# Issuing the value rows' product before the bias rows' product, so that another engine empties the PSUM buffer that q's product takes

## The chip, the cores and the metric

One core of one Trainium2 chip runs the whole kernel. The metric is the device time of one execution in microseconds. The kernel before has a median of 4380.1 us over 3 runs (4376.23 to 4390.58).

## The reference: what is computed

The input `x` has shape (2, 128, 256, 256). One layer does two things to it.

```python
x = x + conv_ref(ln_over_channels(x), W_qkv, W_out, rel_height, rel_width)
t = to_tokens(x)
t = t + ffn_ref(ln_over_channels(t), router_w, router_b, expert_w, expert_b)
x = from_tokens(t)
```

`conv_ref` is windowed attention with 4 heads of 32 channels. q, k and v are 1x1 projections. Each window of 8x8 queries sees 12x12 keys around it. A fixed mask of minus infinity keeps only the pairs whose offset is even in both directions, so the image falls apart into four planes (even and odd rows, even and odd columns) that never mix. The scores get a relative position bias made of q times two small tables. After the softmax the result goes through `W_out`. `ffn_ref` is a mixture of 8 linear experts: a softmax router picks the best two for each token, and the token's output is their weighted sum.

## The kernel before, in words

**Tiling.** A strip is 8 image rows, and there are 64 strips in the two images. A strip has 4 planes of 512 queries, so a main loop of 256 planes (`for n in range(n_planes + 7)`) does nearly all the work. In step `n` the loop scores, attends and projects plane `n`, prepares plane `n + 1` (function `project`, called `ahead` in the loop), and runs the expert layer and the norms for image rows of neighbouring strips. The order of the work on all engines is written out by hand under `tc.manual_schedule`; each engine takes its instructions in that order.

**The TensorE order of one step**, with the lines of the profile: bias scores and q-k scores of plane n (L474, L491); then for plane n + 1 the bias rows `pu` (L408), the value rows `pv` (L350), the key rows `pk` (L423) and q `pq` (L445); four expert products (L714); softmax sums and attention (L512, L522); norm statistics `plt` (L580); three expert products; the output projection `po` (L550); one more expert product; then padding NOPs (L823) that fill the instruction stream to a multiple of 256, and the next step.

**PSUM buffers.** `pu`, `pv`, `pk`, `pq`, `plt`, `plg` and `po` all come from `mm_tile`, a pool of 3 buffers that are handed out in turn. In nearly all steps there are seven of them, so each takes the buffer of the third before it and must wait until that one has been read. In the first strip of each image the value and key rows come in two parts each, which makes nine.

| tile | read by | who next takes its buffer, before |
|---|---|---|
| `pu` | VectorE transpose to `uT`, L413 | `pq` |
| `pv` | ScalarE copy to `vr`, L358 | `plt` |
| `pk` | ScalarE copies to `kcol`, L434 and L441 | `plg` (written by VectorE, L589) |
| `pq` | ScalarE copy to `qs`, L447 | `po` |
| `plt` | VectorE transpose to `plg`, L589 | the next `pu` |
| `plg` | VectorE, last in L621 | the next `pv` |
| `po` | VectorE add, L555 | the next `pk` |

**The VectorE order of one step**, from `uT`: `uT` (L413), two shifted copies and a transpose (L392, L397), `xs` (L699), six expert multiplications (L705), the sum of the finished experts (L720, reads `acc`), softmax sums `sT` (L532, waits for L522), reciprocal, `rT`, `o` (L542), `plg` (L589), the norm chain (L232 to L235, a round trip through ScalarE, L238, L239), the residual add (L555), the router (L613 to L645), and the gate transpose `gT` (L651), which stands just ahead of the next `uT`.

**GpSimd** does, once in a step, a copy that ties it to VectorE's work (L709), an expert multiplication (L705), the norm of one row pair (L276, needs `rb` from a DMA), in every fourth step the halo copy (L250), and a second expert multiplication (L705).

**ScalarE and SyncE, around the change.** ScalarE's order is the router's exponential (L618), a one-element copy into `gb` for expert 5 (L686), the softmax exponential (L499), `vr` (L358), a one-element copy into `gb` for expert 7 (L686), `kcol` (L434, L441), `qs` (L447), and squares (L574). The one-element copies in L686 pace the DMA queue: the DMA that fills `gb` (L689) cannot be issued before its copy is done. SyncE issues nearly all DMAs, in order: `gb` of experts 5 and 7 (L689), `gd` from `gT` (L659), `vrows` from `vr` (L369), `rb` (L665, reads what `gd` wrote), `sb` (L694), `vwin` (L381), and further `gb` loads.

Of the kernel before, what the change touches and what calls it, by code (L numbers as in the profile page):

```python
# [51 lines left out]
def kernel(  # L52
# [39 lines left out]
    def mm_tile(name):  # L92
        return ps_mm.tile([P, 512], F32, tag="mm", name=name)
# [148 lines left out]
    def ln_rows(i):  # L242

        s = strips[i][1]
        return range(1 if s == 0 else 2, KR - 1 if s == NS - 1 else KR)
# [13 lines left out]
    def runs(i, rows):  # L259

        out = []
        for k in rows:
            if out and place(i, k) == out[-1][1] + out[-1][2]:
                out[-1][2] += 1
            else:
                out.append([k, place(i, k), 1])
        return out
# [71 lines left out]
    def value_rows(n):  # L339

        i, pl = divmod(n, 4)
        xp = xn[i % 2][:, pl // 2, pl % 2]
        rows, sent = list(ln_rows(i)), []
        for part in (rows[-4:], rows[:-4]):
            if not part:
                continue
            pv = mm_tile(f"pv{n}_{part[0]}")
            m = len(part)
            for j, k in enumerate(part):
                nc.tensor.matmul(  # L350
                    pv[:, j * P : (j + 1) * P],
                    lhsT=xp[:, k, 1 : PC + 1],
                    rhs=wv,
                    start=True,
                    stop=True,
                )
            vr = work.tile([P, 4, P], F32, tag="vr", name=f"vr{n}_{part[0]}")
            nc.scalar.copy(  # L358
                vr[:, 0:m].rearrange("p r c -> p (r c)"), pv[:, : m * P]
            )  # L360
            sent.append((part, vr))
        return sent
# [23 lines left out]
    def shift(uT, n, state):  # L386

        for j in range(2):
            shifted = uT[:, :, :, NU * j + 3 : NU * j + 9]
            dims = [list(d) for d in shifted.ap]  # L390
            dims[1 + j][0] -= 1
            nc.vector.tensor_copy(  # L392
                auT[n % 2][:, :, :, 6 * j : 6 * j + 6],
                bass.AP(shifted.tensor, shifted.offset, dims),
            )
        au = work.tile([P, 2 * NP, PR, 4], F32, tag="au", name=f"au{n}")
        nc.vector.transpose(au.rearrange("p m a s -> p a s m"), auT[n % 2])  # L397
        state["au"] = au

    def project(n, state):  # L400

        i, pl = divmod(n, 4)
        xp = xn[i % 2][:, pl // 2, pl % 2]
        inner = xp[:, 1 : 1 + PR, 1 : PC + 1]
        kk = kcol[pl]

        pu = mm_tile(f"pu{n}")
        nc.tensor.matmul(pu, lhsT=wrel, rhs=inner, start=True, stop=True)  # L408
        state["sent"] = value_rows(n)
        yield  # L410

        uT = work.tile([P, PR, 4, 32], F32, tag="uT", name=f"uT{n}", bufs=1)
        nc.vector.transpose(uT, pu.rearrange("p (a m s) -> p a s m", a=PR, s=4))  # L413
        state["shift"] = lambda: shift(uT, n, state)
        yield

        rows = list(ln_rows(i))
        for part in (rows[-4:], rows[:-4]):
            if not part:
                continue  # L420
            pk = mm_tile(f"pk{n}_{part[0]}")
            m = len(part)
            nc.tensor.matmul(  # L423
                pk[:, : m * PC],
                lhsT=wk,
                rhs=xp[:, part[0] : part[0] + m, 1 : PC + 1],
                start=True,
                stop=True,
            )
            pk3 = pk[:, : m * PC].rearrange("p (r c) -> p r c", r=m)  # L430
            for k, at, m in runs(i, part):
                new = pk3[:, k - part[0] : k - part[0] + m]
                places = kk[:, :, 0:NK].rearrange("p t (c r) -> p t r c", r=KR)[:, :, at : at + m]
                nc.scalar.copy(places[:, 1 : NP - 1], windows(new[:, :, KC - 3 :], 0, NP - 2))  # L434

                ends = [places[:, 0, :, 1:], new[:, :, 0 : KC - 1]]
                for j, step in enumerate(((NP - 1) * SLOT - KR, PC - KC + 1)):
                    dims = [list(d) for d in ends[j].unsqueeze(1).ap]
                    dims[1] = [step, 2]
                    ends[j] = bass.AP(ends[j].tensor, ends[j].offset, dims)  # L440
                nc.scalar.copy(*ends)  # L441
        yield

        pq = mm_tile(f"pq{n}")
        nc.tensor.matmul(pq, lhsT=wq, rhs=inner, start=True, stop=True)  # L445
        qs = work.tile([P, 2 * NP, PR, 4], F32, tag="qs", name=f"qs{n}")
        nc.scalar.copy(  # L447
            qs.rearrange("p m a s -> p a m s"), pq.rearrange("p (a m s) -> p a m s", a=PR, s=4)
        )
        yield  # L450

        state.update(qs=qs, kk=kk, vv=vwin[n % 2])
        yield

    def windows(rows, n0, count):

        first = rows[:, :, 8 * n0 : 8 * n0 + KC].unsqueeze(1)
        dims = [list(d) for d in first.ap]
        dims[1] = [8, count]
        return bass.AP(first.tensor, first.offset, dims)  # L460
# [317 lines left out]
    for _ in project(0, states[0]):  # L778
        pass
# [28 lines left out]
    with tc.manual_schedule(engines={ET.PE, ET.DVE, ET.Activation, ET.Pool, ET.SP}):  # L808
        for n in range(n_planes + 7):
# [6 lines left out]
            if n + 1 < n_planes:  # L816
                states[n + 1] = {}
                ahead = project(n + 1, states[n + 1])
# [143 lines left out]
```

## Time and profile before

| | |
|---|---|
| median of 3 runs | 4380.1 us |
| the profiled execution, device time | 4380.58 us |
| its span, first to last instruction | 4378.8 us |
| granted TensorE clock, mean | 0.993 |
| TensorE matmul busy, share of the span | 97% |
| TensorE weight loads busy | 56% |
| VectorE busy | 88% |
| ScalarE busy | 33% |
| GpSimd busy | 25% |
| DMA queue q1, share of 16 engines' span | 74.8% |

The durations in this document are from that one profiled execution, which is within 0.5 us of the median. Busy shares are means over the span. The end of a matmul in a profile is modelled, and matmuls overlap, so a busy TensorE row can hide idle time. A wait in the view of waits is a stretch in which an engine stood idle, with the instruction that let it go on.

### The profile page before, as it was taken

The numbers are of one execution on the slowest core, as the hardware profiler recorded it, in microseconds if no ns is written. First come the engines' busy times: TensorE is split into PE (matmuls) and PEld (weight loads), VectorE is DVE, ScalarE is ACT, GpSimd is POOL, SyncE is SP. The second block draws the span as 40 slices with busy tenths as digits, with TensorE's granted clock in tenths as the row PEclk, the third lists the DMA queues.
The fourth block names the chain that finished last, engine by engine and source line by source line (L and its number), as shares of the span: only waits on it lengthen the run. The fifth ranks groups of instructions, "written<-read, shape, count | busy, mean of one in ns | idle before, by whom it ended". The sixth has DMA issues, their size and how long they took to land. (4 is left out here: it accounts for less than half of the span.)

```text
span 4378.8 us, 224652 instructions
## 1 busy us (share of the span) xinstructions
PE 4248.2 (97%) x94273; PEld 2454.2 (56%) x94273; DVE 3853.9 (88%) x11850; ACT 1456.6 (33%) x3774; POOL 1091.6 (25%) x1126
## 2 busy tenths in 40 slices
PE   7899999999999999999999999999999999999987
PEld 5455555555555555555555555555555555555553
DVE  5899889899888989989888889988998888999987
ACT  3333333333333333333333333333333333333321
POOL 1222222222222222222222222222222222222211
PEclk9999999999999999999999999999999999999999
DMA  4677778777777787777777787777777777777766
GB/s 114 210 240 240 244 235 243 241 237 244 233 244 240 244 244 233 243 232 244 238 241 234 240 244 236 243 236 243 238 240 243 236 242 232 244 238 239 243 191 191
DMA packets 824580, 1022.19 MB, mean 233 GB/s; under 512 B 137634, under 2 KB 409634, under 8 KB 823594
## 3 DMA queue, kind: packets, MB, share of 16 engines
q1 hardware_dynamic: 822864, 1007.52, 74.8%
q8 instruction: 769, 12.60, 1.2%
q14 instruction: 217, 1.78, 0.1%
q10 hardware_dynamic: 730, 0.29, 0.0%
HBM read 863.78 MB, written 143.75 MB: 230 GB/s over the span
## 5 line engine op out<-in xcount | busy, mean ns | idle before, releaser
L714 PE MATMUL acc<-xe,ew 128*128 128x512 f32 x4096 | 1916.8, 600 | 21.4 <-DVE gb L688 17.5
L714 PEld LDWEIGHTS acc<-xe,ew 128*128 128x128 f32 x4096 | 757.9, 190 | 941.4 <-issue 872.1
L705 DVE TENSOR_TENSOR xe<-xs,gb 128x512 f32<-128x512 f32 x1536 | 950.5, 686 | 11.8 <-DMA gb<-gd 1.4
L709 POOL COPY last<-xe 128x1 f32<-128x1 f32 x256 | 47.0, 184 | 3088.0 <-DVE gb L688 3081.0
L705 POOL TENSOR_TENSOR xe<-xs,gb 128x512 f32<-128x512 f32 x512 | 650.7, 1272 | 0.7 <-issue 0.5
L276 POOL TENSOR_TENSOR xn<-xt,rb 128x512 f32<-128x512 f32 x249 | 373.7, 1501 | 170.4 <-DMA rb<-gd 164.1
L491 PE MATMUL att<-qs,kcol 32*64 32x32 f32 x32768 | 398.2, 227 | 5.1 <-issue 5.1
L491 PEld LDWEIGHTS att<-qs,kcol 32*64 32x64 f32 x32768 | 395.9, 131 | 6.6 <-issue 6.2
L522 PEld LDWEIGHTS att<-pT,vwin 64*32 64x32 f32 x32768 | 350.2, 105 | 50.4 <-issue 11.8
L522 PE MATMUL att<-pT,vwin 64*32 64x32 f32 x32768 | 350.6, 200 | 8.0 <-issue 6.3
L350 PEld LDWEIGHTS pv<-wt,xn 128*128 128x128 f32 x2048 | 270.1, 192 | 126.5 <-issue 78.7
L434 ACT COPY kcol<-pk 128x560 f32<-128x560 f32 (+2 forms) x344 | 319.0, 927 | 52.8 <-PE pk L423 49.4
L499 ACT ACTIVATE pT<-att 128x1024 f32<-128x1024 f32 x256 | 261.8, 1023 | 208.0 <-PE att L491 207.2
L445 PE MATMUL pq<-xn,wt 128*128 128x512 f32 x512 | 274.7, 617 | 30.0 <-DVE uT L413 26.0
L574 ACT ACTIVATE sq<-xt 128x512 f32<-128x512 f32 x505 | 291.9, 629 | 0.0
L408 PE MATMUL pu<-xn,wrel 128*128 128x512 f32 x512 | 291.7, 651 | 0.0
L397 DVE STREAM_TRANSPOSE au<-auT 128x512 f32<-128x512 f32 x256 | 272.3, 1064 | 9.0
L550 PE MATMUL po<-o,wt 128*128 128x512 f32 x512 | 264.4, 598 | 8.4 <-DVE o L542 5.8
L350 PE MATMUL pv<-wt,xn 128*128 128x128 f32 x2048 | 271.2, 275 | 0.8 <-issue 0.8
L532 DVE STREAM_TRANSPOSE sT<-att 128x512 f32<-128x512 f32 x256 | 183.5, 717 | 98.7 <-PE att L522 84.7
L423 PE MATMUL pk<-xn,wt 128*128 128x512 f32 (+2 forms) x528 | 262.9, 582 | 1.3 <-DVE uT L413 1.3
L474 PEld LDWEIGHTS att<-au,keys 32*64 32x64 f32 x8192 | 117.9, 133 | 227.8 <-PE po L550 183.5
(2696 smaller groups left out, 4895.9 us busy)
## 6 DMA issues: line engine op xcount, KB each, us to landing
gb<-gd SPq DMA_DIRECT2D x2048, 256.0 KB, 5.8
vwin<-vrows SPq DMA_DIRECT2D x512, 240.0 KB, 5.4
xt<-in_x_dram SPq DMA_DIRECT2D x256, 256.0 KB, 6.6
sb<-gd SPq DMA_DIRECT2D x256, 256.0 KB, 4.1
out_dram<-xt SPq DMA_DIRECT2D x256, 256.0 KB, 6.2
rb<-gd SPq DMA_DIRECT2D x249, 256.0 KB, 3.4
vrows<-vr SPq DMA_DIRECT2D x168, 256.0 KB, 3.9
vrows<-vr SPq DMA_DIRECT2D x160, 128.0 KB, 3.5
```

The source lines that it names most:

```text
L276: eng.tensor_tensor(xn[i % 2][:, :, :, k, 1 : PC + 1], ln1_src(i, k).rearrange("p (y j x) -> p y x j", y=2, x=2), rb.rearrange("p (y j x) ...
L350: nc.tensor.matmul(pv[:, j * P : (j + 1) * P], lhsT=xp[:, k, 1 : PC + 1], rhs=wv, start=True, stop=True,)
L397: nc.vector.transpose(au.rearrange("p m a s -> p a s m"), auT[n % 2])
L408: nc.tensor.matmul(pu, lhsT=wrel, rhs=inner, start=True, stop=True)
L434: nc.scalar.copy(places[:, 1 : NP - 1], windows(new[:, :, KC - 3 :], 0, NP - 2))
L445: nc.tensor.matmul(pq, lhsT=wq, rhs=inner, start=True, stop=True)
L491: nc.tensor.matmul(sc[rows, h, 32 * t : 32 * t + 32], lhsT=kk[hp, half * HP + t, :], rhs=qs[hp, m0 : m0 + 2].rearrange("p m a s -> p (m a ...
L522: nc.tensor.matmul(av[hp, half, 32 * t : 32 * t + 32], lhsT=vv[rows, t, hp], rhs=pT[rows, h, 32 * t : 32 * t + 32], start=True, stop=True,)
L550: nc.tensor.matmul(po, lhsT=wo, rhs=state["o"].rearrange("p f z -> p (f z)"), start=True, stop=True)
L574: nc.scalar.activation(sq, src, AF.Square)
L705: eng.tensor_tensor(self.xe[e], self.xs, self.gb.pop(e), ALU.mult)
L714: nc.tensor.matmul(self.acc, lhsT=ew[:, e, :], rhs=self.xe.pop(e), start=(e == 0), stop=not self.xe)
```

## The change

`project` issues the four value-row products, and the ScalarE copy of them that `value_rows` issues, ahead of the bias rows' product. Nothing else is changed: every instruction is still there, with the same operands, and all other instructions keep their order on their engines.

```diff
@@ project
+        state["sent"] = value_rows(n)
         pu = mm_tile(f"pu{n}")
         nc.tensor.matmul(pu, lhsT=wrel, rhs=inner, start=True, stop=True)
-        state["sent"] = value_rows(n)
         yield
```

The turn of the buffers moves with the order of the tiles. Now `pv` takes the buffer of the previous step's `plt`, `pu` that of `plg`, `pk` that of `po` as before, `pq` that of `pv`, and `plt` that of `pu`. In the first strip of an image, with nine tiles, `pq` still takes the buffer of `pu`.

## The prediction

> **What bounds the kernel now.** I read the shares first. The page's first part names two candidates:
>
> ```profile
> PE 4248.2 (97%) x94273; PEld 2454.2 (56%) x94273; DVE 3853.9 (88%) x11850; ACT 1456.6 (33%) x3774; POOL 1091.6 (25%) x1126
> ```
>
> PE looks full, but the view of waits shows both engines waiting for each other (columns: total us, times, longest):
>
> ```profile
> PEld pq L445 <- DVE uT L413: 176.7, 235, 2.0
> DVE sT L532 <- PE att L522: 84.7, 150, 3.7
> POOL xn L276 <- DMA rb<-gd: 164.1, 116, 30.5
> ```
>
> Neither bounds alone. q's product waits for VectorE's `uT`, and later in the step `sT` waits for TensorE's attention. I then took the starts of the rows of 240 middle planes; from `uT` to `uT` they need 16.65 us on average.
>
> TensorE waiting for nothing: q to L512 4.38, to L522 0.455, to its end 1.34, to `po` 3.62, to L474 1.81, scores 2.015, bias and value rows 1.855 (less 0.07 overlap), keys 0.86: **16.27**. Small holes that are no wait for another engine (ahead of L512 7.9 us, in L522 15.7, in L491 8.5, over 240 planes) make it **16.40**.
>
> VectorE waiting for nothing: `uT` to the end of L720 7.02, to `sT` 0.12, `sT` to the next `uT` 8.97: **16.11**. But that last stretch is 0.32 longer on average (call it e). Nearly all of e is in L235, which takes 0.16 us alone and up to 1.25. Its row shows why; here is one plane, by time (start us, us, engine, line):
>
> ```profile
> 728.33 0.58 ACT L358 COPY vr<-pv 128x512 f32<-128x512 f32 x1 [0.92 <-PE pv L350]
> 728.48 0.67 DVE L413 STREAM_TRANSPOSE uT<-pu 128x512 f32<-128x512 f32 x1
> 728.81 0.19 ACT L686 COPY gb<-onesm 128x1 f32<-128x1 f32 x1
> ...
> 729.45 1.21 SPq L659 DMA_DIRECT2D gd<-gT  x2
> ...
> 733.11 0.33 SPq L665 DMA_DIRECT2D rb<-gd  x1
> ...
> 736.71 1.51 POOL L276 TENSOR_TENSOR xn<-xt,rb 128x512 f32<-128x512 f32 x1 [0.29 <-DMA rb<-gd]
> ...
> 738.17 1.27 POOL L705 TENSOR_TENSOR xe<-xs,gb 128x512 f32<-128x512 f32 x1
> ...
> 738.99 0.47 DVE L235 SCALAR_TENSOR_TENSOR u__42_13603<-u__42_13603,epsc 128x8 f32<-128x8 f32 x1
> ```
>
> L235 ends with POOL's L705 (739.46 and 739.44): POOL is late, because `rb` was late, because `gd` was issued at 729.45 although `gT` was done at 728.55. SP takes its DMAs in order, and ahead of `gd` stands the `gb` of expert 7, which waits for ScalarE's copy behind `vr`. SP's own waits say the same for the whole span:
>
> ```profile
> SPq L689 <- ACT gb L686: 852.2, 525, 16.0
> SPq L659 <- DVE gT L651: 39.6, 11, 11.5
> ```
>
> `gd` hardly ever waits for `gT`. So `vr`, and thus `pv`, sets when `rb` comes.
>
> **What the Trainium skill says.** *Perfetto Trace Analysis*, Identifying the Most-Contended Engine: matmul busy time is no measure of TensorE's headroom, weight loads are better. The trace agrees: 97% against 56%, and the PE row hides most of q's wait. *SBUF — State Buffer*, Who interferes with whom: a VectorE instruction with two SBUF inputs and a GpSimd one that reads SBUF exclude each other for the whole instruction. L235 agrees (0.16 to 1.25 us, ending with POOL). *Perfetto Trace Analysis*, Identifying Dependency Chains: an instruction that waits for several engines may get an event-semaphore instruction ahead of it. `po` has that (255 of 51 ns).
>
> **The loop as it stands, checked.** If TensorE leads the pace, attention ends, `sT` follows after 0.14, and `uT` 8.97 + e later; from the scores' end s this is s + 1.67 + e. q starts 0.73 after `uT` began and, started cold, needs 13.73 to the next s. So the next s is s + 16.13 + e, against 16.27 by TensorE alone: VectorE delays TensorE when e passes 0.14. The mean of what passes is 0.24, and 16.40 + 0.24 = **16.64**; measured 16.65. The account closes.
>
> **The change, part by part.**
>
> *q no longer waits for `uT`.* q then waits for `vr`. That copy can start when the softmax exponential ends, s + 1.2, and ends near s + 1.8; q's turn is at s + 2.65. No wait, with 0.8 to spare. The stall itself, q's start less its turn, was 43.7 us over 240 planes, and the cold start 0.11 in half of them: 12.3. That is 0.23 per plane or 60 us at most. The cold weight load now falls on `pv`, where `pu` paid it before: nothing.
>
> *`pu` moves behind `pv`.* Eight products of 0.11 put it 0.89 later: it starts at s + 0.82, ends near s + 1.95, and `uT` starts not before s + 2.0. Before, 58% of the planes had `uT` under 0.93 after `pu`, so here is the price: a new wait at L413. What is queued behind it is VectorE's whole chain to `sT`. Taken alone it is 0.16 per plane on average. It does not add where TensorE leads, since `sT` waits less by as much.
>
> *The new loop.* VectorE from `uT` s + 2.0 reaches `o`'s end 9.62 later. NOPs follow `o`: first at 0.16, 31 of them in 2.26, then 0.07 to the scores and 2.015 to their end, so s is not before `uT` + 14.13. With `uT` = s + 1.84 + e in a late plane, the next s is s + 15.97 + e. VectorE now delays TensorE only when e passes **0.30** instead of 0.14.
>
> *`vr` comes 0.9 earlier*, and with it, on ScalarE and SP, the copy for expert 7, its `gb`, and `gd`. `gd` was issued on average 1.08 after `uT`'s start; now `gT` holds it, about 0.3. The same trace shows what that is worth: in the 47 planes where `gd` went out within 0.79 of `uT`'s start, POOL waited 0.08 for `rb`, in the others 0.47. The `vrows` DMA stands behind `gd` and moves with it; `rb`, `sb`, `vwin` follow, none later than before.
>
> *e afterwards.* `sT` is hardly late any more, so e has to be taken from the earliest `sT`. For those 47 planes it is then 0.10 without the halo copy and 0.64 with it (every fourth plane), and what passes 0.30 is 0.03 and 0.34. Mean 0.75 x 0.03 + 0.25 x 0.34 = 0.11.
>
> *Edits at no cost.* `plt` now waits for `uT` as well as for ScalarE's squares, so I expect an event semaphore there; at 51 ns it is between nothing and 13 us over 256 planes. I take nothing, since TensorE's sequencer runs ahead there, and one padding NOP less (71 ns) returns it. `pu` waits for L621, which ends 2.6 before `uT`, as `pv` did. `pv` waits for L589, over 4 us earlier, as `pu` did. The 8 planes with nine tiles keep q's wait. The holes in TensorE wait for nothing that the trace shows, so I can't say that they stay; 32 us in all, they may grow or shrink by a sixth: plus or minus 5 us.
>
> *Sum.* 16.40 + 0.11 = 16.51 against 16.65: 0.14 x 256 = 36 us. From the profiled execution's 4380.6 (0.5 from the median): **4345 us**.
>
> **The rivals.**
>
> - *TensorE sets the pace alone.* Halo planes are absorbed too: 16.40, 0.24 x 256 = 62, so 4318. For: all of q's stall goes. Against: 0.64 passes 0.30. Chance 0.2.
> - *No change.* `gd` is earlier, but `rb` only partly, since the DMA engines are 75% full. If half of the planes behave like the early ones and half like the late ones (0.37 passes 0.30 there, from the earliest `sT`), it is 0.5 x 0.11 + 0.5 x 0.37 = 0.24, the loss of before: 4380. Chance 0.13.
> - *Slower, by GpSimd's end.* `rb` does not come earlier at all. With `sT` no longer late, L235 reaches POOL sooner and waits longer, and the wait for `pu` comes on top. What passes 0.30, over all 236 planes with POOL rows, would be 0.31 in place of 0.24: 0.055 x 256 = 14, so 4394. It decides from the point where over half of the planes have `rb` as late as now. For: `rb` follows `gd`'s issue by 2.7 us with a wide spread. Against: the 47 planes. Chance 0.17.
> - *It doesn't do what it says* is only true of the 8 planes with nine tiles.
>
> My forecast has 0.5. **Range**: 4318 to 4394 reaches to the cases at both ends and takes in the event semaphores and the holes; beyond it lie about half of each end case, some 2 in 10. A difference of 0.3% (13 us) is about what this measurement tells from none. Faster 0.5 + 0.2 = 0.7, same 0.13, slower 0.17.
>
> **What would show it.** Right: q's waits for `uT` nearly gone (under 20 us); `sT` <- L522 under 30; a new `uT` <- `pu` of 20 to 60 beside the 35 at the start; SP's wait for ScalarE's `gb` down by over 100 and its wait for `gT` up; POOL's `rb` wait under 90; L235 long only in every fourth plane; 255 or so event semaphores at L580. Wrong: POOL's wait for `rb` as before, or q waiting for `vr`, or larger holes ahead of L512.

## The result: 56 us less, and the profile after

The kernel after takes 4323.6 us (median of 4 runs, 4316.7 to 4327.1) against 4379.5 us of the kernel before, run on the same chip (4 runs). The ratio is 0.9866, with a 95% interval of 0.9844 to 0.9888. The profiled execution took 4321.7 us (span 4319.9) at a granted clock of 0.992.

The direction came as forecast, and so did what frees q and what makes `gd` early. The size did not: the gain was 56 us, where the forecast had 36 and the rival "TensorE sets the pace alone" 62.

The page's first part, after:

```profile
PE 4217.3 (98%) x94273; PEld 2466.8 (57%) x94273; DVE 3852.5 (89%) x11850; ACT 1452.8 (34%) x3774; POOL 1086.0 (25%) x1126
```

The instructions are the same in number. VectorE's busy time differs by 1.4 us and ScalarE's by 3.8. TensorE's matmul row is 30.9 us shorter with as many products, which fits a row that had hidden a part of q's wait. So the gain lies in waits. The view of waits, after (total us, times, longest):

```profile
PEld pq L445 <- issue: 115.4, 480, 0.3
POOL xn L276 <- DMA rb<-gd: 74.6, 15, 29.7
DVE uT L413 <- PE pu L409: 63.6, 39, 13.9
...
DVE sT L532 <- PE att L522: 16.3, 19, 2.3
...
ACT vr L358 <- PE pv L350: 9.7, 8, 4.4
```

- q's weight load no longer waits for `uT` (176.7 us before). What is left has no releaser: 480 gaps of about a quarter of a microsecond, nearly two in each step.
- `sT` waits 19 times for the attention, where it waited 150 times.
- GpSimd's waits for `rb` fell from 116 to 15.
- The forecast price is there too: `uT` now waits 63.6 us for `pu`, 28 more than before.
- `vr` no longer waits for `pv` (241.0 us before, in 254 planes). It starts when ScalarE is free.

The lines of before for the last two points:

```profile
ACT vr L358 <- PE pv L350: 241.0, 254, 5.2
...
DVE uT L413 <- PE pu L408: 35.3, 13, 12.3
```

SyncE's waits, after:

```profile
SPq L689 <- ACT gb L686: 784.2, 675, 14.5
...
SPq L659 <- DVE gT L651: 54.1, 59, 9.7
```

`gd` (L659) is held by `gT` in 59 steps, where it was held in 11. The step that the prediction showed, by time (start us, us, engine, line):

```profile
725.35 1.02 PE L409 MATMUL pu<-xn,wrel 128*128 128x512 f32 x2
...
725.55 0.58 ACT L358 COPY vr<-pv 128x512 f32<-128x512 f32 x1
...
726.03 0.19 ACT L686 COPY gb<-onesm 128x1 f32<-128x1 f32 x1
...
726.28 0.24 DVE L651 STREAM_TRANSPOSE gT<-g 128x64 f32<-128x64 f32 x1
...
726.66 1.43 SPq L659 DMA_DIRECT2D gd<-gT  x2
...
734.37 1.50 POOL L276 TENSOR_TENSOR xn<-xt,rb 128x512 f32<-128x512 f32 x1
...
735.84 1.26 POOL L705 TENSOR_TENSOR xe<-xs,gb 128x512 f32<-128x512 f32 x1
...
736.75 0.38 DVE L235 SCALAR_TENSOR_TENSOR u__42_13603<-u__42_13603,epsc 128x8 f32<-128x8 f32 x1
```

`vr` is copied while `pu` is computed. So ScalarE's copy for expert 7 is done at 726.22, before `gT` (726.52), and `gd` goes out 0.14 after `gT`, where it was 0.90. GpSimd's L276 then shows no wait for `rb`, and L235 takes 0.38 in place of 0.47, although it still ends with GpSimd's L705 (737.13 and 737.10).

From the row starts of 236 middle planes, as means: `gd` goes out 0.18 after `uT`'s start (1.13 before), GpSimd waits 0.04 for `rb` (0.38), and a plane takes 16.386 us (16.65). That is 0.264 x 236 = 62 us; the span is 59 us shorter, so the planes at the two ends gained nothing.

### The profile page after: what moved, and what is told of

It is laid out like the page before. It is cut to its first block, busy times and chain, and to the rows that moved or that the text cites. A ratio compares the mean times of both kernels' runs of the same rounds, so it can differ in the third digit from the quotient of the medians.

```text
span 4319.9 us, 224653 instructions
## 1 busy us (share of the span) xinstructions
PE 4217.3 (98%) x94273; PEld 2466.8 (57%) x94273; DVE 3852.5 (89%) x11850; ACT 1452.8 (34%) x3774; POOL 1086.0 (25%) x1126
## 5 line engine op out<-in xcount | busy, mean ns | idle before, releaser
L714 PE MATMUL acc<-xe,ew 128*128 128x512 f32 x4096 | 1915.4, 600 | 18.6 <-DVE gb L688 16.5
L705 DVE TENSOR_TENSOR xe<-xs,gb 128x512 f32<-128x512 f32 x1536 | 950.6, 686 | 11.1 <-DMA gb<-gd 1.1
L705 POOL TENSOR_TENSOR xe<-xs,gb 128x512 f32<-128x512 f32 x512 | 650.6, 1272 | 1.5 <-PE att L522 0.7
L491 PE MATMUL att<-qs,kcol 32*64 32x32 f32 x32768 | 400.6, 226 | 11.1 <-issue 10.8
L491 PEld LDWEIGHTS att<-qs,kcol 32*64 32x64 f32 x32768 | 396.7, 131 | 13.9 <-issue 13.6
L276 POOL TENSOR_TENSOR xn<-xt,rb 128x512 f32<-128x512 f32 x249 | 373.7, 1501 | 91.1 <-DMA rb<-gd 74.6
L522 PEld LDWEIGHTS att<-pT,vwin 64*32 64x32 f32 x32768 | 348.6, 105 | 40.8 <-issue 3.2
L522 PE MATMUL att<-pT,vwin 64*32 64x32 f32 x32768 | 345.1, 200 | 2.4 <-issue 2.2
L350 PE MATMUL pv<-wt,xn 128*128 128x128 f32 x2048 | 301.1, 291 | 0.9 <-issue 0.9
L409 PE MATMUL pu<-xn,wrel 128*128 128x512 f32 x512 | 266.2, 602 | 1.2 <-issue 1.2
L445 PE MATMUL pq<-xn,wt 128*128 128x512 f32 x512 | 261.9, 592 | 0.9 <-issue 0.8
L350 PEld LDWEIGHTS pv<-wt,xn 128*128 128x128 f32 x2048 | 251.7, 193 | 11.8 <-issue 1.3
L474 PEld LDWEIGHTS att<-au,keys 32*64 32x64 f32 x8192 | 118.9, 132 | 234.0 <-PE po L550 181.1
L413 DVE STREAM_TRANSPOSE uT<-pu 128x512 f32<-128x512 f32 x256 | 177.1, 692 | 65.5 <-PE pu L409 63.6
```

The lines of the kernel that those rows point to most:

```text
L276: eng.tensor_tensor(xn[i % 2][:, :, :, k, 1 : PC + 1], ln1_src(i, k).rearrange("p (y j x) -> p y x j", y=2, x=2), rb.rearrange("p (y j x) ...
L350: nc.tensor.matmul(pv[:, j * P : (j + 1) * P], lhsT=xp[:, k, 1 : PC + 1], rhs=wv, start=True, stop=True,)
L491: nc.tensor.matmul(sc[rows, h, 32 * t : 32 * t + 32], lhsT=kk[hp, half * HP + t, :], rhs=qs[hp, m0 : m0 + 2].rearrange("p m a s -> p (m a ...
L522: nc.tensor.matmul(av[hp, half, 32 * t : 32 * t + 32], lhsT=vv[rows, t, hp], rhs=pT[rows, h, 32 * t : 32 * t + 32], start=True, stop=True,)
L705: eng.tensor_tensor(self.xe[e], self.xs, self.gb.pop(e), ALU.mult)
L714: nc.tensor.matmul(self.acc, lhsT=ew[:, e, :], rhs=self.xe.pop(e), start=(e == 0), stop=not self.xe)
```

## The experiments

The theory to test was that the gain needs **both** things that the new order brings, q's product free of `uT`, and `vr`, thus `gd` and `rb`, early. The two rivals were that one of them alone is enough. A further question was what sets the pace now. All ratios are to the kernel before on the same chip (medians there 4377.2 to 4379.5).

The readings, as means or sums over 236 middle planes. The last two columns are the gaps in TensorE ahead of two instructions, to which the last section returns; they are sums of start-to-start times over 0.12 us. The time is the median of all runs of a kernel; the other columns come from its one profiled execution, which for e4 (4343.3 us) and e6 (4380.6 us) is the fastest of its runs. That is why e6's plane is shorter than that of before while its median is longer. Where the text below compares stages of TensorE, these are means over the same planes from start to start.

| kernel | time, us | ratio, 95% | plane | `gd` after `uT` | `rb` wait | 18th q-k product | 108th attention product |
|---|---|---|---|---|---|---|---|
| before | 4379.5 | | 16.65 | 1.13 | 0.38 | 8.9 | 18.1 |
| after | 4323.6 | 0.9844–0.9888 | 16.386 | 0.18 | 0.04 | 13.9 | 4.3 |
| e3 | 4341.0 | 0.9903–0.9934 | 16.487 | 0.15 | 0.01 | 37.0 | none |
| e4 | 4351.9 | 0.9928–0.9965 | 16.502 | 0.87 | 0.18 | 5.9 | 25.9 |
| e5 | 4361.7 | 0.9938–0.9973 | 16.569 | 1.03 | 0.33 | 10.6 | 15.6 |
| e6 | 4386.3 | 1.0010–1.0025 | 16.628 | 0.22 | 0.02 | 16.5 | 0.2 |
| e7 | 4354.8 | 0.9932–0.9968 | 16.563 | 0.17 | 0.01 | 46.4 | 0.1 |
| e9 | 4338.7 | 0.9890–0.9930 | 16.467 | 0.42 | 0.04 | 20.6 | 3.1 |
| e11 | 4373.3 | 0.9975–0.9999 | 16.621 | 1.04 | 0.42 | 3.0 | 37.0 |

### Request and issue apart: e1 and e2

The change does two things in one line: it requests `pv`'s PSUM tile first, and issues its products first. e1 requests first only; e2 issues first only. Both take the tiles out of `value_rows` into a function of their own.

```diff
 e1:
+        pvs = value_tiles(n)
         pu = mm_tile(f"pu{n}")
         nc.tensor.matmul(pu, lhsT=wrel, rhs=inner, start=True, stop=True)
-        state["sent"] = value_rows(n)
+        state["sent"] = value_rows(n, pvs)
 e2:
         pu = mm_tile(f"pu{n}")
+        state["sent"] = value_rows(n, value_tiles(n))
         nc.tensor.matmul(pu, lhsT=wrel, rhs=inner, start=True, stop=True)
-        state["sent"] = value_rows(n)
```

> The buffers are handed out as in the kernel after (value rows' first, then the bias rows'), but TensorE issues the bias rows' product first, as in the kernel before. So q's product waits for ScalarE's copy vr and not for VectorE's uT, while vr, and with it gd and rb, stay as late as before, and pu stays early. Theory A (loop sums: TensorE's own 16.40 us per plane, plus what of VectorE's lateness e passes the slack of the loop; here the slack is 0.65, since pu is early and the scores are held only through o and the NOPs): 16.45, 4330 us; waits of q for uT near 0, of sT for L522 still some 60 to 90, of POOL for rb 150 as before. Theory B (q's wait for uT alone is the gain): 4324. Theory C (the earlier gd alone is the gain): 4380.

> The other half: TensorE issues the value rows first, as in the kernel after, but pu's buffer is handed out first, so q's product still takes pu's buffer and waits for uT, which now waits for a later pu. vr and gd are early. Theory A: uT not before s + 2.0, q 0.73 later, 13.73 to the next s: 16.46 plus holes 0.13, and in halo planes more: 16.73, 4400 us; q waits for uT in nearly every plane, POOL's wait for rb falls to 80 or so. Theory B: 4380 or more. Theory C: 4324.

e1 took 4377.7 us, ratio 1.0 [0.9987, 1.0012]; e2 took 4318.2, ratio 0.9873 [0.9847, 0.9898]. Neither pulled the two apart. In e1 q still waits for `uT` (178.3 us in 232 planes), in e2 it doesn't. That is what comes of it if a tile gets its buffer in the order of the first writes, not of the requests. So e1 behaves as the kernel before over again and e2 as after over again, and as separations both failed; what was expected of them stays untested there. They serve as repeats: no change in one, 60 us less in the other.

### Buffers named by hand: e5, e6, e7

To force the separation, each tile of `mm_tile` gets a buffer by its turn of request:

```diff
-        return ps_mm.tile([P, 512], F32, tag="mm", name=name)
+        return ps_mm.tile([P, 512], F32, tag=f"mm{next(mm_turn) % 3}", name=name, bufs=1)
```

e6 has this with the request and issue of e2: `gd` early, q on `pu`'s buffer. e5 has it with those of e1: q on `pv`'s buffer, `gd` late.

> TensorE issues the value rows first, so vr and gd are early as in the kernel after, but the buffers are named by hand so that q's product still takes the bias rows' buffer and waits for uT. Theory A: uT starts 2.0 after the scores' end, q 0.73 later and cold, 13.73 to the next scores' end: 16.46 plus holes of 0.12, and more in halo planes: 16.6 to 16.7, 4365 to 4395 us. Theory B: 4378 or more. Theory C: 4322.

> The pool gives a buffer at a tile's first write, not at its request (in the profiles of e1 and e2, q waits as in the kernel of the same issue order), so here the three buffers are named by hand, in the order of requests: value rows' tile first, then the bias rows'. TensorE still issues the bias rows first. So q's product takes the buffer that ScalarE empties, and nothing else is changed: vr, gd and rb are as late as before. Theory A (loop sums): q waits for nothing (vr ends 0.04 to 0.1 us before its turn), VectorE's lateness has a slack of 0.65 and passes it by 0.05: 16.45 us per plane, 4330 us. Theory B (q's wait alone is the gain): 4322. Theory C (the earlier gd alone is the gain): 4378, with the time of q's wait turning up at another place.

**e6** took 4386.3 us, ratio 1.0018: 8 us slower than before, and the gain is gone, as theory A had it (4365 to 4395). Its waits:

```profile
PEld pq L451 <- DVE uT L419: 204.1, 248, 1.3
...
DVE uT L419 <- PE pu L415: 107.9, 190, 14.1
...
POOL xn L278 <- DMA rb<-gd: 72.8, 8, 32.8
```

and one step by time:

```profile
2014.58 0.72 DVE L419 STREAM_TRANSPOSE uT<-pu 128x512 f32<-128x512 f32 x1 [0.24 <-PE pu L415]
...
2015.35 0.30 PEld L451 LDWEIGHTS pq<-xn,wt 128*128 128x128 f32 x2 [0.78 <-DVE uT L419]
...
2015.35 1.13 PE L451 MATMUL pq<-xn,wt 128*128 128x512 f32 x2
```

`rb` is as early as in after, so this is the one-cause test of the buffer. `pu` is later, `uT` waits for it in 190 planes, and q waits behind both in 248. Of the 0.242 us that a plane takes more than in after, 0.161 lie between the key rows and q and 0.088 between q and L512, so it is q's wait and not the naming of the buffers that costs. **Early `rb` alone, in the new order, is worth nothing.**

**e5** gained only 16 us. Its waits:

```profile
PEld pq L452 <- ACT vr L364: 158.3, 248, 0.6
POOL xn L278 <- DMA rb<-gd: 148.7, 100, 29.2
...
DVE sT L539 <- PE att L529: 71.4, 113, 3.7
```

q is free of `uT` but now takes the buffer that the *late* `vr` empties: its weight load waits in 248 planes and starts cold. From q's start to L512 it takes 4.50 instead of 4.38. I had expected about 4330; I had left out that `vr` itself is late when `pv` is issued second. A second cost came with it: `pu` now takes the buffer of `plg`, and the stretch from the scores to the bias rows grew from 0.147 to 0.191. e7 adds the early `gd` to e5 (the edit of e3 below).

> e5 with the one-element copy for expert 7's gb ahead of vr on ScalarE, as in e3: q is free of uT, gd is early, the bias rows stay first. Both gains of the kernel after without its later pu. Theory A: TensorE alone sets the pace, 16.265 plus holes of 0.12 to 0.2: 16.39 to 16.46, 4315 to 4332 us. Theory B and C: 4322 each, since this has both.

It took 4354.8 us, ratio 0.995 [0.9932, 0.9968], not the 4315 to 4332 expected of both together.

```profile
PEld pq L452 <- ACT vr L364: 158.2, 248, 0.6
...
DVE sT L539 <- PE att L529: 122.2, 220, 3.7
...
POOL xn L278 <- DMA rb<-gd: 80.0, 9, 29.3
...
PEld att L498 <- issue: 37.2, 62, 1.7
```

`rb` is early, but q still waits for `vr` (4.47 to L512), and a gap ahead of one q-k product has grown to 46.4 us. Against after's 16.386 that makes 0.09 (cold q) + 0.12 (both gaps, (46.5 - 18.2) / 236) = 0.21; the path from `po` to the scores returns 0.03 (1.811 against 1.838), and 0.18 was measured. So the two effects can't be had by pinning buffers in the old order: **issuing `pv` first is what makes q's new buffer early.**

### `gd` early in the kernel before: e3 and e9

```diff
-            next(ahead, None)
             nxt.fetch(7, nc.scalar)
+            next(ahead, None)
```

The copy for expert 7 now stands ahead of `vr` on ScalarE. Nothing changes on TensorE, and q keeps `pu`'s buffer.

> The kernel before, with one thing moved: ScalarE's one-element copy for expert 7's gb stands ahead of the copy vr in place of behind it, so SP can issue gd as soon as gT is done. q still waits for uT, the order of TensorE is that of before. Theory A: e is that of the planes with an early gd (0.06 without halo copy, 0.62 with it), the slack stays 0.14: 16.40 + 0.75 x 0.03 + 0.25 x 0.48 = 16.55, 4353 us. Theory B: 4380. Theory C: 4324. POOL's wait for rb 60 to 90 in A and C.

e3 took 4341.0 us, 37 less than before: better than theory A (4353), and not all that theory C forecast (4324). Its waits:

```profile
DVE sT L532 <- PE att L522: 103.8, 213, 3.7
PEld pq L445 <- DVE uT L413: 100.8, 213, 1.3
POOL xn L276 <- DMA rb<-gd: 82.2, 12, 30.2
DVE uT L413 <- PE pu L408: 42.5, 19, 13.3
...
PEld att L491 <- issue: 29.7, 58, 1.6
```

`rb`'s wait is gone but for 12 times, and most of q's with it, since VectorE is no longer late: q's start lags its turn by 0.022 us. (The view shows 100.8 us, but it counts all idle time ahead of q's weight load, and in after 115.4 us of that stand there without any wait.) That shows that `gd`'s place on SyncE's queue was what made `uT` late. Expert 7's `gb` itself, which comes earlier too, is no rival: in before VectorE's multiplications waited 1.4 us in all for such a DMA, and GpSimd's had 0.7 us of idle time of any kind.

Against after a plane takes 0.101 more. By stages of TensorE, the q-k products take 0.089 more, with the gap ahead of the 18th; the stretch from the bias and value rows to L512, with what is left of q's wait, 0.050; the attention gives back 0.015 and the path from `po` to the scores 0.028. So **an early `gd` alone, in the old order, has about two thirds of the gain**, and most of what is lacking is the gap, not q's wait. The theory that both things are needed does not hold in the old order. e9 puts two idle ScalarE copies (128x128, 0.30 us each) ahead of expert 7's, to see whether that gap follows the time of `gd`:

```diff
+                nc.scalar.copy(idle, onesm)
+                nc.scalar.copy(idle, onesm)
             nxt.fetch(7, nc.scalar)
             next(ahead, None)
```

> e3 (order of before, the one-element copy for expert 7's gb ahead of vr) with two idle copies of 128x128, together some 0.6 us, ahead of that copy, in time that ScalarE spends waiting for pv. So gd goes out some 0.5 us later than in e3 and still earlier than in the kernel before: measured from the scores' end, about 2.3 us as in the kernel after, in place of 1.8 (e3) and 3.1 (before). Theory E (the holes in TensorE at the 18th q-k product, 37 us in e3 and 46 in e7 against 9 in before and 14 in after, come from where the DMAs that follow gd fall against TensorE's own time): the hole falls to 10 to 20 us and the time to 4318 to 4335. Theory F (the holes come with pu first and rb early, whatever the DMAs' place): hole 35 or more, and the time is e3's 4341 or a little over, since rb comes later.

The gap fell to 20.6 us, but the time only to 4338.7 [0.989, 0.993], which can't be told from e3. Inconclusive: the q-k products gained 0.065 a plane, but the key rows to q and q to L512 each took 0.019 more and the attention 0.008.

### `gd` late again in the kernel after: e4 and e11

Three (e4) or four (e11) idle copies hold up ScalarE behind `vr`:

```diff
             next(ahead, None)
+                nc.scalar.copy(idle, onesm)      # 3 times in e4, 4 times in e11
             nxt.fetch(7, nc.scalar)
```

> The kernel after, with three idle copies of 128x128 (about 0.75 us together) on ScalarE between vr and the one-element copy for expert 7's gb, so that gd goes out about as late as in the kernel before. They lie in time that ScalarE spends waiting for pk. q is still free of uT. Theory A: VectorE's lateness, taken from the earliest sT, passes the slack (0.30 by my sum, 0.48 with uT to o as measured in the kernel after) by 0.21 to 0.31: 16.61 to 16.71, 4370 to 4395 us: nearly all of the gain gone. Theory B: 4324. Theory C: 4380.

> e4 with four idle copies (1.2 us) in place of three, so that gd goes out 1.15 us after uT's start, as late as in the kernel before (1.13), against 0.87 in e4 and 0.18 in the kernel after. q's product stays free. Theory A: POOL's wait for rb is that of before (0.38 a plane, e4 0.18, after 0.04) and the time goes up with it: 4365 to 4385 us, no gain left or nearly none. Theory B (a free q is worth something by itself, as the 16 us of e5): 4350 to 4362.

e4 gave 4351.9, between the expectations. Counted from `uT`'s start, `gd` was only partly late there (0.87). e11 made it nearly as late as before (1.04) and gave 4373.3, ratio 0.9987 [0.9975, 0.9999]; nearly all of the gain is gone. The waits, e4's line first, then e11's:

```profile
POOL xn L276 <- DMA rb<-gd: 102.0, 68, 29.2
```

```profile
POOL xn L276 <- DMA rb<-gd: 164.0, 126, 30.0
...
PEld pq L445 <- issue: 71.9, 300, 0.2
DVE uT L413 <- PE pu L409: 59.7, 35, 13.2
...
DVE sT L532 <- PE att L522: 35.0, 50, 2.7
PEld att L522 <- issue: 31.4, 77, 1.5
```

In e11 q has no wait for `uT`, and GpSimd waits for `rb` as in before. But "as late as before" has two readings. Counted from the end of the scores, `gd` goes out after 3.10 us in before, 2.33 in after, 3.10 in e4 and 3.47 in e11, where `uT` itself is later. By this count e4 is after with the `gd` of before, and it keeps 26 of the 56 us; by the count from `uT`, and by GpSimd's wait, it is e11, which keeps 4. So q's freedom alone is worth between 4 and 26 us, with e5's 16 in between: "q's freedom is enough" fell, and "it is worth nothing alone" is not shown.

Nor is all of the loss VectorE's lateness. By stages of TensorE, a plane of e11 takes 0.235 more than one of after: 0.085 are in the two columns of gaps (0.128 more in the attention, 0.043 less in the q-k products) and 0.039 between q and L512, where the last section finds a gap of the same kind; 0.113 are VectorE's, since `o` ends 11.98 after the scores and not 11.62 (0.038 ahead of `po`, 0.075 between `po` and the scores). In e4 the shares are 0.075 and 0.042. So late `gd` costs in two ways. e11's idle copies also make ScalarE's later copies 0.10 later (e4's don't). The one wait for them in the view, 38.8 us ahead of q's weight load, is the usual gap there and costs nothing: from the key rows to q e11 takes 0.860, after 0.857.

### What sets the pace now: e8, e10, e12

e8 moves the halo copy of every fourth step behind GpSimd's second multiplication; e10 moves the padding NOPs from ahead of the scores to ahead of the output projection, so that they no longer follow `o`; e12 does both.

```diff
 e8:
-            if pl == 3 and i + 2 < len(strips):
-                halo(i + 2)
             nxt.times(7, pool)
+            if pl == 3 and i + 2 < len(strips):
+                halo(i + 2)
 e10:
-            if 6 <= n < n_planes:
+            if n == 6:
                 nc.tensor.addr_align(BLOCK, offset=BLOCK - FIRST_LIMIT)
...
+            if 6 <= n < n_planes - 1:
+                nc.tensor.addr_align(BLOCK, offset=BLOCK - FIRST_LIMIT - 9)
             next(outp, None)
```

> The kernel after, with GpSimd's halo copy (every fourth plane) behind its second expert multiplication in place of ahead of it, so that GpSimd is done 0.63 us earlier in those planes and L235 waits less. Theory A (in the kernel after TensorE alone sets the pace, VectorE's lateness stays within its slack): 0 to 8 us off, 4314 to 4322. Theory D (VectorE and GpSimd still set it in every fourth plane, where uT to uT is 16.77 against 16.26): 0.5 us in 64 planes, 32 us off, 4290.

> The kernel after with the padding NOPs placed ahead of the output projection in place of behind it, the pieces of 256 instructions starting at the same instructions. So after o TensorE's sequencer no longer has 31 NOPs (2.26 us) to pass before the scores. Theory A (the NOPs are what VectorE's lateness reaches TensorE by): the wait between po and the scores, 0.028 us a plane, goes, and what it held up: 5 to 12 us off, 4310 to 4318. If the NOPs don't matter: 4322. If the NOPs now hold up the output projection (they end before o in nearly all planes): 4322 or more.

> The kernel after with both moves: the halo copy last on GpSimd (e8) and the padding NOPs ahead of the output projection (e10). Theory A (TensorE's own instructions set the pace; NOPs and halo copy no longer reach it): 16.265 plus holes of 0.1: 4308 to 4318, the same as e10 within the measurement.

e8: 4319.5 us, ratio 0.9862 [0.9844, 0.9881]. In after, `uT` to `uT` takes 16.77 in the halo planes and 16.26 in the others; in e8 16.36 and 16.39. The bump is gone, the mean is the same (16.383). e10: 4312.4, 0.9848 [0.9828, 0.9868], a plane 16.392; the path from `po` to the scores fell from 1.838 to 1.811, and the plane didn't follow. e12: 4315.6, 0.9853 [0.9837, 0.9868], a plane 16.396. What e8 and e10 take off VectorE's last lateness, 0.022 and 0.027 a plane between `po` and the scores, comes back elsewhere on TensorE (in e10 0.013 ahead of `po` and 0.007 in each kind of scores). So it brings nothing that can be measured: **TensorE's own instructions, with the gaps between them, set the pace of after.** e10's median is the lowest of all, but its interval overlaps that of after, and its mean plane is not shorter; a version that beats after is not shown.

## Why the prediction was right, and where it was not

- **q's stall.** Right: the wait is gone. e6 shows that q's new buffer was needed once `pv` goes first, since `pu` and with it `uT` are later then. In the old order an early `gd` takes most of the stall away as well (e3), which the prediction did not consider.
- **The price at `uT`.** Right: 28 us more of `uT` <- `pu` (20 to 60 forecast, beside the 35 at the start), and it did not lengthen the plane.
- **`gd` and `rb`.** Right: 0.18 after `uT` (about 0.3 forecast), GpSimd's wait 0.04 and 74.6 us in all (under 90). Late `gd` costs 28 us (e4) to 50 (e11) of the gain, and early `gd` is worth 37 us where q keeps its buffer (e3). The rivals "no change" and "slower, by GpSimd's end", both built on a late `rb`, fell with this.
- **SyncE's wait.** Its wait for ScalarE's `gb` fell by 68 us only, not by over 100. That of `gd` for `gT` rose, as said. The other one-element copies stayed where they were.
- **The term that was mis-sized** is the path from `uT` to `o`'s end, "9.62", in *The new loop*. It measures 9.41 to 9.46. I had taken it with `sT` starting after a semaphore wait, 0.12 or more behind L720's end. Without one, `sT` starts on average 0.04 *before* the recorded end of L720. The slack is therefore near 0.48, not 0.30. The lateness of the halo planes (0.61 to 0.64, forecast 0.64) passes 0.48 by 0.13 to 0.14 in one plane of four, 0.03 on average instead of 0.11, and when e8 takes it away the plane is only 0.006 shorter. With the holes, TensorE alone makes 16.265 + 0.02 (ahead of L512) + 0.014 (L522) + 0.055 (L491) = 16.35; what VectorE's lateness still adds, between `po` and L474, is 0.028: 16.38, against 16.386 measured. That is the first rival's arithmetic but for the 0.028. It was given the smaller chance on the ground that "0.64 passes 0.30". The range took the result in; the forecast's own sum, with 0.11 for VectorE, fell short.
- **e afterwards.** L235 was to be long only in every fourth plane. It is over 0.2 in 170 of the 178 planes without the halo copy too: mean 0.51 against 0.42 over all, and 0.91 with the halo copy. The reason is the same 0.2: `sT` and all behind it come earlier, while GpSimd's L705 ends 10.64 after `uT` (median without the halo copy), as it did in the planes of before with an early `gd` (10.63), and L235 lasts to that end. This agrees with the Trainium skill, *SBUF — State Buffer*, Who interferes with whom, on instructions that exclude each other for their whole length. The longer wait absorbs part of what VectorE had gained, and costs nothing, since TensorE leads.
- **The event semaphore at L580** did not come: there are 8, as before, and 31 padding NOPs as before. The Trainium skill's *Perfetto Trace Analysis*, Identifying Dependency Chains, says that several producers *may* bring one. No run here showed an added one at L580.
- **The holes.** They were left open by 5 us either way. In the two columns of the table they fell by 9 us (27.0 to 18.2), and in e3, e7 and e11 they moved by more. In the loop's sum they are 0.09 in place of 0.135. A plane gained 0.264 where 0.14 was forecast: 0.08 of the 0.124 between them come from the mis-sized term, about 0.045 from the holes, to which the prediction had given no sign.
- **Two small slips.** In the third rival 0.31 less 0.24 is 0.07 as printed, not 0.055, which puts its end at 4398. And `gd` went out 1.13 after `uT` in before, not 1.08. Neither bears on the outcome.

## What to carry to other kernels

Before a rotation of buffers is changed, ask of each tile not only who empties its new buffer but when that emptier itself can start: moving the producer made q's wait disappear, renaming the buffer alone (e5) traded it for another. When one engine's copy paces an in-order DMA queue, the transfers behind it are late by that copy; one moved line in e3 was worth 37 us with no change in TensorE's instructions. When a kernel has two ways out of a wait, try the smaller one alone: here the earlier DMA by itself, with no buffer changed, had about two thirds of the gain. And when a slack is worked out, take each stretch from steps in which its wait is absent, since 0.2 us in the slack decided here between two forecasts.

## What the runs showed of the hardware that I had not expected

The gaps in TensorE that "wait for nothing" are not spread out. Nearly all of those in the scores and the attention stand ahead of two fixed instructions: the 18th q-k product and the 108th attention product. Counted from the step's start these are instructions 99 and 611, in a step of 768. The hole ahead of L512 stands at a third, instruction 355, in the second expert product (2.6 us of it in after, 5.7 in before, 9.7 in e11, beyond the usual 0.43 from start to start). The three are 256 apart. Queue q8, listed on the page as the instruction queue, moves 769 packets of 16 KiB in every kernel here, three in a step, about 1.1 us each:

```profile
q8 instruction: 769, 12.60, 1.3%
```

The times of these packets in the traces tell what the gaps wait for. Where there is a gap, the product behind it starts a nearly fixed time after the last packet of q8 has landed. At the 18th q-k product this is 1.38 us in the 23 steps of after with a gap over 0.2, 1.37 in 61 of e3 and 1.41 in 62 of e7; at the 108th attention product it is 1.38 in 77 steps of e11. The spread is about 0.1 everywhere. In the steps without a gap the packet had landed earlier, on average 2.79, 2.42, 2.45 and 1.73 us before. So these are gaps at which instructions arrive late.

When the packet lands differs between kernels with the same instructions on TensorE. The third packet of a step starts 2.67 us after instruction 611 in after, but 3.30 in e3 and 3.33 in e7, which have the large gaps at the 18th; the second starts 0.41 after instruction 355 in after, but 0.96 in e4 and 1.10 in e11, which have them at the 108th. The table has the same pattern: where `gd` is late (before, e4, e5, e11: 0.87 to 1.13) the larger gaps are at the 108th, 15.6 to 37.0 us; where it is early (after, e3, e6, e7, e9) they are at the 18th, 13.9 to 46.4. That the DMAs behind `gd` hold up one or the other packet is a guess that agrees with this; no run separated it from the rest, and the one that tried, e9, was inconclusive.
